# A recurrence block on one core: other durations in the books of the planner that orders its instructions

## The chip, the core and the metric

The kernel runs on one core of one Trainium2 chip, as one program with one launch. The metric is the device time of the execution in microseconds (us); the time before is the median of three runs. A profile is one further execution, taken by the hardware profiler.

## What is computed

The reference takes x of shape 8 x 1024 x 128 and applies two layers, each as `x = x + layernorm(layer(layernorm(x)))`. The first is a gated recurrence with 16 heads, keys of 64 and values of 128:

```
q, k, v = silu(causal_conv4(x @ W.T))          # per head; q, k then divided by their length
alpha   = exp(-exp(A_log) * softplus(x @ Wa.T + dt_bias));  beta = 2 * sigmoid(x @ Wb.T)
each token:  S = alpha * (S - beta * k (k S)) + k v ;  o = q S
result  = rms_norm(o) @ Wo.T
```

The second is a small feed-forward: two mixes of the token with the one before it, `sigmoid(mix_r @ W_r.T) * (square(relu(mix_k @ W_k.T)) @ W_v.T)`. All of it is in float32.

## The kernel before

**Tiling.** A unit is one batch entry (8), one half of its 1024 tokens (2) and one group of four heads (4): 64 units. A unit has four chunks of 128 tokens. Within a chunk the recurrence is written as matrix products: products of k with k and with q, weighted with decays (`products`, line 876); the inverse of a 128 x 128 triangular matrix for each head and chunk, 16 in a unit, made in blocks of 16 on GpSimd (`blocks`, line 957) and then from 16 to 32, 64 and 128 on TensorE, VectorE and ScalarE (`levels`, line 1002); and, chunk after chunk, the update of the state S (`prepares`, line 1119, and `steps`, line 1157). Ahead of this stand the normalisation of x and the gates (`begins`, 603), the projections with their convolutions (`conv`, 700, used by `keys`, 732, and `values`, 797) and the lengths of q and k (`lengths`, 740). Behind it stand the norm of the output with squares that accumulate (`norms`, 1233), the output projection (`projects`, 1263) and the second layer (`ending`, 1299).

**What sets the order.** All of these are generators, called streams, 17 in all. A stream runs to its next `yield part(...)`, which names the engine of the part that follows, the tiles that it reads, and the buffers and PSUM banks that it takes. `Flow.run` (line 177) holds the next part of each stream. For each it works out from its own books the time at which the part could start: the later of its engine's clock, of its operands' times plus SLACK (0.65) and of the time at which the buffers are free. Of those that could start within NEAR (0.35) of the earliest it takes the one of the lowest step number, and its instructions are issued. So the planner runs while the program is built, and what it leaves is a fixed order of instructions on each engine. On the chip each engine takes its instructions in that order, and waits where an operand isn't there.

The books are `Engine.cost` (line 245), which gives a duration for each instruction, and `Flow.note` (line 125), which moves the engine's clock on by it and marks when tiles were written and read. For TensorE the cost also has two shares of use, from which `Flow.clock` (line 106) works out windows in which TensorE's clock is halved; in such a window `run` puts parts with a low share off (YIELD). A DMA is booked with 3.0 us and half a microsecond of its queue (ISSUE). No number of the books reaches the program except through the order.

**PSUM.** Two tiles of two banks (pair) and four of one bank (bank) serve all products. A group of products writes one of them; the next group mostly writes another.

**The chain of the inverse.** `gathers` (line 936) writes the diagonal blocks of 16 of mt to DRAM in eight DMAs (md), and reads them back with the factors (cb, nb). `blocks` first multiplies nb with cb and then runs 28 small operations with tmp and nb on GpSimd. `scatters` (line 982) sends the result through DRAM (td) into tq, from which `levels` starts. In `levels` the tile x64 (x in the profile) is made on VectorE and tt on ScalarE. GpSimd also fills the first three columns of pb for the convolutions, whose taps follow on VectorE as acc.

Every instruction that the planner issues is recorded at line 234, the one call in `emit`, so the profile's groups are told apart by the names of their tiles. A float32 matmul leaves two records and a transposition one, so four products show as x8.

Of the kernel before, what the change touches and what calls it, by code (L numbers as in the profile page):

```python
# [22 lines left out]
NB = CU * G  # L23
# [11 lines left out]
class Flow:  # L35
# [11 lines left out]
    NEAR = 0.35  # L47
    SLACK = 0.65
    ISSUE = 0.5
    WINDOW, SLEEPS, WAKES = 3.4133, 0.475, 0.75  # L50

    def __init__(self, nc):
        self.now = dict(PE=0.0, DVE=0.0, ACT=0.0, POOL=0.0, SP=0.0)
        self.free, self.wrote, self.read = {}, {}, {}
        self.kinds, self.work = {}, [0.0, 0.0]
        self.of = {}
        self.speed, self.window, self.used = 1.0, self.WINDOW, [0.0, 0.0]
        self.pe, self.ve = Engine(self, "PE", nc.tensor), Engine(self, "DVE", nc.vector)
        self.ac, self.po = Engine(self, "ACT", nc.scalar), Engine(self, "POOL", nc.gpsimd)
        self.sp = Engine(self, "SP", nc.sync)  # L60
# [45 lines left out]
    def clock(self, t, cost, use):  # L106

        left = cost
        while True:
            while self.window <= t:  # L110
                if self.speed == 1.0:
                    if self.used[0] < self.SLEEPS * self.WINDOW:
                        self.speed = 0.5
                elif self.used[1] >= self.WAKES * self.WINDOW:
                    self.speed = 1.0
                self.used = [0.0, 0.0]
                self.window += self.WINDOW
            if left < 1e-6:
                return t
            d = min(left / self.speed, self.window - t)  # L120
            left -= d * self.speed
            self.used = [u + d * k for u, k in zip(self.used, use)]
            t += d

    def note(self, eng, op, outs, ins, cost):
        t = self.now[eng]
        for ap in ins:
            t = max(t, self.last(self.wrote, ap, eng))
        for ap in outs:
            if ap.space != DRAM:  # L130
                t = max(t, self.ends(ap, eng))
        if eng == "PE":
            self.now[eng] = self.clock(t, *cost)
            self.work = [self.work[0] + cost[0], self.work[1] + cost[0] * cost[1][1]]
            end = self.now[eng] + 0.1 + 0.1 / self.speed
        elif eng == "SP":
            self.now[eng] = t + self.ISSUE
            end = t + cost
        else:
            self.now[eng] = end = t + cost  # L140
        for ap in ins:
            self.mark(self.read, ap, end, eng)
        for ap in outs:
            self.mark(self.wrote, ap, end, eng)
# [79 lines left out]
class Engine:  # L224
# [20 lines left out]
    def cost(self, op, outs, ins, args, kw):  # L245
        def size(ap):
            n = 1
            for k in list(ap.shape)[1:]:
                n *= k
            return n  # L250

        n = size(outs[0])
        if self.name == "PE":

            if op == "transpose":
                return 0.109, (0.88, 0.88)
            k, m = ins[0].shape[0], size(ins[0])
            if n <= 4:
                return (0.08 if n == KW - 1 else 0.223), (0.0, 0.0)
            if k <= 32 and m <= 32:  # L260
                return 0.011 + 0.0005 * n, (0.0, 0.0)
            if k <= 64 and m <= 64:
                return 0.105, (0.64, 0.04)
            if m <= 32:
                return 0.25, (0.5, 0.2)
            t = max(0.223, n * 0.00168)
            return (t, (1.0, 1.0)) if k > 64 and m > 64 else (0.58 * t, (1.0, 0.58))
        if self.name == "DVE":
            if op == "tensor_tensor_scan":
                return 0.23 + 0.00204 * n  # L270
            if op == "bn_stats":
                return 0.28
            if op == "bn_aggr":
                return 0.18
            if op == "tensor_scalar" and n == P:
                return 0.38
            if op == "scalar_tensor_tensor":
                return 0.23 + (0.00117 if all(ap.space != PSUM for ap in ins) else 0.00104) * n
            return 0.155 + 0.00104 * n
        if self.name == "ACT":  # L280
            if "accum_out" in kw:
                return 0.174 + 0.0008 * n + 0.23
            if n == TU and op == "activation":
                return 0.69 if kw.get("scale") is not None else 0.63
            return 0.175 + 0.0008 * n
        if self.name == "POOL":
            if ALU.pow in args:
                return 0.41 + 0.166 * n
            if op == "memset":
                return 0.12  # L290
            if op == "tensor_scalar":
                return 0.25 + 0.0009 * n
            return 0.33 + 0.0018 * n
        return 3.0
# [1131 lines left out]
```

## Time and profile before

| | |
|---|---|
| median of 3 runs | 3776.48 us (3766.68 to 3783.44) |
| the profiled execution's own time | 3780.87 us |
| its span, first to last instruction | 3779.1 us |
| mean granted TensorE clock | 0.949 of full speed |
| HBM read and written | 138.18 MB and 23.07 MB, 43 GB/s over the span |
| DMA, mean of its largest queue | 22.9% of 16 engines' span |

The busy time of an engine is the time in which at least one of its instructions was executing, and its share is of the span. The chain of waits starts at the last instruction and goes back, at each step, to what released it; its shares add up to the span. An entry such as "DVE acc" stands for VectorE (DVE) writing the tile acc; ACT is ScalarE, POOL is GpSimd, SP is SyncE, which issues the DMAs, and PE is TensorE. A timeline's row gives the start and the length in us, the engine, the operation, the tile written and those read, the count of records, and in brackets the idle time of the engine before it with what ended it.

### The profile page before, as it was taken

To read this page: it belongs to the slowest core of one execution; us is meant where nothing else is said; L and a number is where in the kernel's file an instruction comes from. 1 tells how busy PE (TensorE), PEld (TensorE's weight loads), DVE (VectorE), ACT (ScalarE), POOL (GpSimd) and SP (SyncE) were. 2 spreads that over 40 slices of the span, in tenths; PEclk is the share of its full clock that TensorE was granted. 3 is DMA by queue.
4 is the path that set the end of the run, shared out by engine and by line. 5 is a ranking of instruction groups with operands and counts; after the bars stand their busy time and mean duration, and the time that the engine had idled before them with its cause. 6 is when DMAs were issued, how large, how long until landed. Compare 5 with 4: busy or idle time off the path is not lost.

```text
span 3779.1 us, 126912 instructions
## 1 busy us (share of the span) xinstructions
PE 3435.4 (91%) x52848; PEld 2646.7 (70%) x52848; DVE 2688.5 (71%) x5021; ACT 2311.7 (61%) x5779; POOL 2404.3 (64%) x4369
## 2 busy tenths in 40 slices
PE   6899998999999999998998989999998989989996
PEld 3677776777777776776766767767776767667775
DVE  5776767677777777866777677777767777777752
ACT  4566656666657666666656656566565666566652
POOL 4666667567666666666566566666666656576662
PEclk8899999999999999999999999999999989999997
DMA  3221222222222222221222222222222222222210
GB/s 80 56 53 39 54 45 49 54 45 55 49 55 46 57 50 43 56 53 40 54 44 53 52 42 53 47 54 51 51 45 55 49 41 60 44 48 53 49 39 11
DMA packets 713151, 186.28 MB, mean 49 GB/s; under 512 B 573152, under 2 KB 679040, under 8 KB 712576
## 3 DMA queue, kind: packets, MB, share of 16 engines
q1 hardware_dynamic: 712576, 178.17, 22.9%
q8 instruction: 415, 6.80, 0.8%
q14 instruction: 160, 1.31, 0.1%
HBM read 138.18 MB, written 23.07 MB: 43 GB/s over the span
## 4 chain that ended last, share of the span: by engine, by line
PE 63%; DVE 10%; POOL 7%; ACT 7%; SPq 6%; issue 5%; DMA 3%; POOLq 0%; DVEq 0%; ACTq 0%
PE bank L234 38%; PE pair L234 25%; SPq L234 6%; DVE acc L234 5%; POOL nb L234 3%; POOL tmp L234 2%; DMA nb<-md 2%; ACT acc L234 1%; DVE x L234 1%; ACT tt L234 1%; DVE at L234 1%; ACT L234 1%; ACT pb L234 1%; POOL vr L234 1%; ACT junk L234 1%
## 5 line engine op out<-in xcount | busy, mean ns | idle before, releaser
L234 DVE SCALAR_TENSOR_TENSOR acc<-pb,taps,acc 128x512 f32<-128x512 f32 x1344 | 1076.1, 806 | 158.2 <-POOL pb L234 64.9
L234 POOL TENSOR_TENSOR vr<-vr,r 128x128 f32<-128x128 f32 (+1 forms) x448 | 353.9, 791 | 252.5 <-ACT vr L234 247.0
L234 PE MATMUL bank<-xnT,wT 128*128 128x512 f32 x892 | 492.4, 641 | 14.8 <-ACT tt L234 8.7
L234 POOL TENSOR_TENSOR nb<-nb,tmp 128x14 f32<-128x14 f32 (+6 forms) x896 | 337.8, 377 | 70.2
L234 ACT COPY pb<-bank 128x512 f32<-128x512 f32 x446 | 259.6, 582 | 161.0 <-PE bank L234 122.1
L234 POOL TENSOR_TENSOR qk<-qk,egb 128x256 f32<-128x256 f32 x256 | 228.4, 892 | 202.5 <-PE pair L234 201.4
L234 ACT COPY o<-pair 128x512 f32<-128x512 f32 x256 | 150.4, 588 | 328.3 <-PE pair L234 286.2
L234 POOL TENSOR_TENSOR tmp<-nb 128x14 f32<-128x14 f32 (+6 forms) x896 | 319.4, 356 | 48.4
L234 DVE TENSOR_TENSOR_SCAN at<-at,ident 128x512 f32<-128x512 f32 x256 | 336.5, 1314 | 12.0 <-DMA at<-rowd 11.7
L234 PEld LDWEIGHTS bank<-tn,mt 32*32 32x32 f32 (+1 forms) x14240 | 276.4, 110 | 97.1 <-issue 22.3
L234 ACT ACTIVATE junk<-o 128x128 f32<-128x128 f32 x1024 | 317.5, 310 | 26.4
L234 PE MATMUL bank<-tn,mt 32*32 32x16 f32 (+1 forms) x14240 | 310.0, 190 | 17.8 <-DVE tn L234 7.6
L234 PE MATMUL pair<-vr,tt 128*128 128x128 f32 x2048 | 292.9, 289 | 26.7 <-ACT tt L234 19.5
L234 ACT ACTIVATE acc<-bank,taps 128x512 f32<-128x512 f32 x446 | 309.7, 694 | 0.3
L234 POOL TENSOR_TENSOR so<-so,es 128x4 f32<-128x4 f32 x256 | 64.2, 251 | 377.7 <-ACT junk L234 377.4
L234 PE MATMUL bank<-woT,oT 128*128 128x128 f32 x2048 | 290.1, 285 | 10.5 <-ACT oT L234 7.2
L234 PEld LDWEIGHTS bank<-wv,xnT 128*128 128x128 f32 x2016 | 257.9, 197 | 57.8 <-issue 36.1
L234 POOL TENSOR_TENSOR o<-o,so 128x512 f32<-128x512 f32 x256 | 284.8, 1112 | 18.0
L234 PEld LDWEIGHTS pair<-vr,tt 128*128 128x128 f32 x2048 | 265.9, 203 | 42.6 <-ACT tt L234 22.1
L234 PE MATMUL pair<-w,at 128*128 128x128 f32 x2048 | 291.8, 287 | 0.2 <-issue 0.2
L234 PE MATMUL bank<-wv,xnT 128*128 128x128 f32 x2016 | 284.7, 286 | 7.4 <-issue 3.5
L234 PEld LDWEIGHTS bank<-woT,oT 128*128 128x128 f32 x2048 | 255.2, 194 | 46.0 <-issue 15.9
(202 smaller groups left out, 7739.1 us busy)
## 6 DMA issues: line engine op xcount, KB each, us to landing
at<-rowd SPq DMA_DIRECT2D x256, 256.0 KB, 3.3
egb<-rowd SPq DMA_DIRECT2D x512, 64.0 KB, 3.2
tq<-td SPq DMA_DIRECT2D x256, 64.0 KB, 2.2
tt<-tq SPq DMA_DIRECT2D x256, 64.0 KB, 2.6
md<-mt SPq DMA_DIRECT2D x512, 16.0 KB, 1.8
nb<-md SPq DMA_DIRECT2D x64, 128.0 KB, 2.8
td<-nb SPq DMA_DIRECT2D x128, 64.0 KB, 3.1
xs<-in_L_attn_x_dram SPq DMA_DIRECT2D x16, 256.0 KB, 3.4
```

Source lines behind the costliest of these rows:

```text
L234: res = call(*args, **kw)
```

## The change

Other numbers are put into `Engine.cost`, and `Flow.note` adds a time whenever a TensorE instruction writes another tile than the one before it. The streams, their step numbers and offsets, HOP, SLACK, NEAR, YIELD, the shares of use and the entries of the other operations stay. Here n is the number of columns written and NB is 16.

```diff
@@ class Flow
+    TURN = 0.07
...
+        self.into = None
@@ note
         if eng == "PE":
+            if outs[0].tensor.name != self.into:
+                self.into, t = outs[0].tensor.name, t + self.TURN
             self.now[eng] = self.clock(t, *cost)
@@ cost, TensorE
             if op == "transpose":
-                return 0.109, (0.88, 0.88)
+                return 0.115, (0.88, 0.88)
...
-            t = max(0.223, n * 0.00168)
-            return (t, (1.0, 1.0)) if k > 64 and m > 64 else (0.58 * t, (1.0, 0.58))
+            t = max(0.235, n * 0.00172)
+            return (t, (1.0, 1.0)) if k > 64 and m > 64 else (0.61 * t, (1.0, 0.58))
@@ cost, VectorE, operations without an entry of their own
-            return 0.155 + 0.00104 * n
+            return (0.23 if n <= 2 * NB else 0.155) + 0.00104 * n
@@ cost, ScalarE
             if "accum_out" in kw:
-                return 0.174 + 0.0008 * n + 0.23
+                return 0.174 + 0.0008 * n + 0.33
```

## The prediction

> **What bounds the kernel.** I read the page's spans first, then its slices, its chain of waits, and then the timeline around single idle times of TensorE.
>
> ```profile
> span 3779.1 us, 126912 instructions
> PE 3435.4 (91%) x52848; PEld 2646.7 (70%) x52848; DVE 2688.5 (71%) x5021; ACT 2311.7 (61%) x5779; POOL 2404.3 (64%) x4369
> ...
> PE 63%; DVE 10%; POOL 7%; ACT 7%; SPq 6%; issue 5%; DMA 3%; POOLq 0%; DVEq 0%; ACTq 0%
> ```
>
> The reader is to see that TensorE is the bound but not all of it: it is idle for 3779.1 - 3435.4 = 344 us, and 37% of the chain runs through the other engines and the queues. The mean granted clock, 0.949, hides a third part: the trace's clock is either whole or half, so the half clock held for about 2 x 0.051 x 3779 = 386 us, in 62 stretches, and cost at most 193 us.
>
> TensorE's own work at full clock I add up from paces read as start to next start in the timeline: 4,224 products of 128x128 at 0.223 us, 464 of 128x512 at 0.86, 3,584 with one side 64 at 0.134, 1,024 of 64x256 at 0.258, 2,831 transpositions at 0.109, 13,312 of 32x32 (8,192 at 0.0186, 5,120 at 0.035), 2,048 of 64x64 at 0.10, 256 against the 32-column pair at 0.25 and some 20 us of small ones: 3,014 us. The order has 3,983 changes of the tile written, and four products take 0.893 us without one and 0.987 with: 0.094 each, 374 us. Together 3,388 us. So about 372 us between TensorE's groups are stalls and half clock, and 19 us are start and end. A schedule can win or lose only in the 372 and in the number of changes.
>
> How a stall is made is seen in the timeline of TensorE, VectorE, ScalarE and GpSimd around 1840 us (start, length, then the group; in brackets the idle time before it):
>
> ```profile
> 1839.07 1.02 PE L234 MATMUL bank<-xnT,wT 128*128 128x512 f32 x2
> 1842.50 0.44 PE L234 MATMUL bank<-ident,qk 128*128 128x128 f32 x2 [2.41 <-ACT tt L234]
> ...
> 1846.78 1.92 PE L234 MATMUL pair<-vr,tt 128*128 128x128 f32 x8
> ...
> 1857.12 1.06 PE L234 MATMUL pair<-vr,tt 128*128 128x128 f32 x8
> ```
> ```profile
> 1838.70 2.41 DVE L234 SCALAR_TENSOR_TENSOR acc<-pb,taps,acc 128x512 f32<-128x512 f32 x3 [1.65 <-POOL pb L234]
> 1841.14 0.69 DVE L234 TENSOR_TENSOR x<-bank,cn 64x512 f32<-64x512 f32 x1
> ```
> ```profile
> 1837.32 0.73 POOL L234 TENSOR_TENSOR nb<-nb,cb 128x256 f32<-128x256 f32 x1 [2.04 <-DMA nb<-md]
> ```
>
> Read it from below: GpSimd waits 2.04 us for a DMA; behind it in its queue stands the filling of pb; VectorE's taps wait for pb, and x of the levels stands behind the taps; ScalarE's tt waits for x; TensorE waits 2.41 us. Then the clock is halved: the same eight records take 1.92 us instead of 1.06. An in-order queue that waits for something later than the planner thought is the mechanism, and the DMA's duration in the books (3.0) isn't edited.
>
> **The change, part by part.** No instruction of work is added or removed: both built programs hold the same products, operations, DMAs and table loads; bare waits rise by 24 in all (TensorE -27, VectorE +32, ScalarE +11, SyncE +15, GpSimd -7), at most some 2 us at the 0.07 us that GpSimd's timeline shows between two instructions, and beside other work. I take 0 for them. What moves is the order, everywhere: from the 17th run of TensorE's order on the two differ, and of 7,066 runs 2,702 still follow each other alike. At large nothing moves: TensorE's groups of the recurrence stand on average 2 to 3 us of TensorE work earlier (spread 3), the convolutions 0.3 later; only the gates' products of begins stand 58 us later, which still has begins done ahead of need.
>
> TensorE's entries. Four products: books 0.892 before, 0.94 + 0.07 = 1.01 after, trace 0.987. One of 128x512: 0.860, 0.951, trace 0.97 with the change of tile. Four of one side 64: 0.517, 0.643, trace 0.55 to 0.65. Four transpositions: 0.436, 0.53, trace 0.44 to 0.53. Summed over all instructions the books held 2,962 us for TensorE and hold 3,110 + 3,948 x 0.07 = 3,386 now, against my 3,388. So TensorE's books were 13% short and now are right. The other two entries are less so: a square with accumulator is booked at 0.606 instead of 0.506, while two in a row start 0.43 to 0.44 us apart (1,024 of them, 102 us too much on ScalarE); small VectorE operations of 16 columns go from 0.172 to 0.247, while their rows show 0.163 to 0.253 (384 of them, 29 us). These cost no time themselves; they act through the order alone.
>
> The order. The changes of tile fall from 3,983 to 3,948: 35 x 0.094 = 3.3 us gained. For the stalls I counted, in both orders, how much TensorE work (at the paces above) stands between a group and the last earlier TensorE group on which its operands or its free bank depend, through other engines and everything ahead in their queues. Call it the cover. Set beside the trace of before, the excess time ahead of groups (idle and half clock together) falls with it: 186 groups had under 1 us and lost 129 us, 0.69 each; 431 had 1 to 1.75 us and lost 117 us, 0.27 each; 832 had 1.75 to 2.5 and lost 88, 0.106 each; 2,534 had more and lost 39, 0.015 each. In the new order these counts are 145, 552, 817 and 2,434. So -41 x 0.69 = -28.3, +121 x 0.27 = +32.9, -15 x 0.106 = -1.6, -100 x 0.015 = -1.5: +1.5 us. The worst places get fewer, the middling ones more, as a planner should do that no longer counts TensorE work short: it fits a wait more closely, with less left over.
>
> The DMA chain isn't in that count, since what waits is GpSimd. The cover between the products that feed md and GpSimd's first operation on nb falls from 14.9 to 14.4 us on average over the 64 units. Bounds: nothing, or 0.53 x 64 = 34 us of GpSimd's waiting. I take nothing: in the trace of before the wait on nb doesn't get longer with less cover (correlation +0.2, the wrong sign), since the DMAs stand in SyncE's queue behind others.
>
> At the half clock a rule can be weighed. The trace has 62 half-clock stretches, and ahead of 60 of them TensorE was idle for over 30% of 3.4 us, though only 22 idle times are over 3 us; at 1842.50 one of 2.41 us was enough. My prices per group hold the half clock already, from the rows. The Trainium skill (TensorE: Matmul & The Clock Gate, HAM oscillation) gives as its rule that TensorE should have no idle gaps over some 3.4 us, so that shorter ones would cost only themselves. By it the prices would be those of the groups at full clock, 0.42, 0.185, 0.047 and nothing, and the orders would differ by -17.2 + 22.4 - 0.7 = +4.5 us instead of +1.5; the rows of this trace go against the rule, and the sum goes by the rows.
>
> Sum: -3.3 + 1.5 = -1.8 us on the profiled execution's 3780.9 (span 3779.1 and 1.8 around it): 3779. That execution lies 4.4 us over the median of 3776.5, so I forecast 3775.
>
> **The rivals.** Faster: the groups with 1 to 1.75 us lost 0.27 each because the old books misjudged them; where the new books put 121 more, the work does fit, and they cost nothing. For it: TensorE's sum is now right to 0.1%. Against: the example's stall began at a DMA, not at a wrong product. Then -28.3 - 1.6 - 1.5 - 3.3 = -35: 3742. It is over 0.5% (19 us, about what a measurement here can tell from no change) if such a place costs under 0.13.
>
> Slower: thinner cover over the DMA chain decides. Place: GpSimd's first operation of blocks, behind nb.
>
> ```profile
> POOL nb L234 <- DMA nb<-md: 87.3, 49, 5.5
> ```
>
> It waits in 49 of 64 units already (total, times, longest). DMA nb<-md holds 2% of the chain, 76 us, so 0.87 of that waiting is felt at the end. If the lost cover becomes waiting one for one, 34 x 0.87 = 30 us; and each idle us has drawn 193 / 344 = 0.56 us of half clock: 46 us. With -1.8 that is 3821. It decides for slower by 0.5% as soon as 40% of the 34 us is felt. The correlation speaks against it, the example's timeline for it.
>
> That the change does nothing, because the planner would pick the same, is excluded by the orders.
>
> **How the numbers follow.** Within 0.5%, which is the forecast's own range of 3758 to 3795: 0.36, the likeliest, at 3775, where the places priced by before balance. Slower: 0.34, at 3821 and between, since a tighter order has less in hand for any operation that comes late. Faster: 0.30, at 3742. The price per place is a mean over few: ten more or fewer deep stalls of 1 to 3 us with their half clock are 15 to 45 us, either way. The range takes in both rivals and that spread beyond them by about 15 to 27 us: 3715 to 3835.
>
> **What would show it.** TensorE's busy time less its half clock falls by 3 us and no more. Idle times of TensorE over 1 us, 103 now: about as many if I am right, under 90 in the faster case. The wait of GpSimd on DMA nb<-md, 87.3 us: over 110 in the slower case. The clock stays at 0.945 to 0.953; 0.96 says faster, 0.94 slower. I am wrong if the page shows another engine's share of the chain grow by over 3% of the span, since then a queue that I did not count decides.

## The result, and the profile after

The changed kernel takes **3814.07 us** (median of 4 runs, 3812.62 to 3826.56) beside 3771.87 for the kernel before on the same chip (four runs there, the three of the table and one more): 1.0104 times as long, 95% interval 1.0081 to 1.0128. I had forecast 3775 and no change. The time lies inside the range, 3715 to 3835, but the likeliest case was wrong. The profiled execution took 3812.86 us.

From the page after, the span, the engines and the chain of waits:

```profile
span 3811.1 us, 126936 instructions
PE 3444.4 (90%) x52848; PEld 2644.8 (69%) x52848; DVE 2701.8 (71%) x5021; ACT 2308.7 (61%) x5779; POOL 2421.4 (64%) x4369
...
PE 51%; POOL 13%; DVE 10%; SPq 7%; ACT 6%; issue 5%; DMA 5%; POOLq 0%; DVEq 0%; ACTq 0%
```

The counts of instructions of work are those of before. The span is 32 us longer: TensorE is idle for 23 us more (3811.1 - 3444.4 = 366.7, before 343.7) and busy for 9 more. The half clock isn't the reason: it held for 364 us in 54 stretches (before 388 in 62), and the mean granted clock rose from 0.949 to 0.953.

**Where the time went.** I put both traces on one scale, TensorE's own work done at the full-clock paces of the prediction, and took the difference of the times at which the same amount of work was done. Over the first 2,510 us of work the difference wanders between -15 and +18 us; from 2,420 on it stays between 0 and 10. Over the next 40 us of work, from 2,788 us of time in the kernel after, it jumps by 30; close to the end it stands at +37.8, and the spans differ by 32.0. So the loss that is left at the end has one place. Fifty microseconds around it, in the windows of before and after (length, then busy us of PE, PEld, DVE, ACT, POOL, then granted clock, DMA share and GB/s):

```profile
2755.00:2805.00 50.00, 47.68 (x791) 37.22 (x788) 34.93 (x62) 30.75 (x82) 35.33 (x63) 0.97 0.26 49
```
```profile
2800.00:2850.00 50.00, 35.46 (x563) 23.20 (x559) 39.29 (x55) 24.45 (x50) 33.66 (x71) 0.81 0.28 51
```

TensorE is busy for 35 us there instead of 48, and part of that at half clock. What it lacks is seen from SyncE's queue: the blocks of the inverse of one unit, number 47 of 0 to 63, the last unit of the sixth of eight batch entries. First before, then after:

```profile
2624.26 0.55 SPq L234 DMA_DIRECT2D rowd<-rows  x1
...
2747.03 3.77 SPq L234 DMA_DIRECT2D md<-mt  x8
...
2752.18 0.40 SPq L234 DMA_DIRECT2D nb<-md  x1
...
2773.81 1.33 SPq L234 DMA_DIRECT2D td<-nb  x2
```
```profile
2769.66 0.38 SPq L238 DMA_DIRECT2D rowd<-rows  x1
2771.53 0.33 SPq L238 DMA_DIRECT2D at<-rowd  x1
...
2776.64 3.93 SPq L238 DMA_DIRECT2D md<-mt  x8
...
2783.84 0.52 SPq L238 DMA_DIRECT2D nb<-md  x1
...
2811.70 1.32 SPq L238 DMA_DIRECT2D td<-nb  x2
```

The eight DMAs that carry the unit's blocks start 30 us later than before, though the two traces were at most some 9 us apart in the 75 us of work ahead of that, the result goes out 38 us later, and `levels` starts at 2,821 instead of 2,786. The lines just ahead of the DMAs say why: rowd<-rows writes the decays of the *next* batch entry to DRAM, at<-rowd reads them back, and only then do the products of unit 47's last chunk go. Before, the same write stood 123 us ahead of the unit's DMAs. The longest wait of SyncE's queue in this stretch, 2,690 to 2,830 us (total, times, longest):

```profile
SPq L238 <- DVE rows L238: 24.3, 1, 24.3
```

A long wait there is no sign by itself, since before the queue waited 19.2 us for another tile (cr) in the same stretch; what counts is what stood behind it. TensorE's rows from the gates of the next entry to the starved stretch:

```profile
2718.32 1.87 PE L238 MATMUL bank<-wabT,xnT 128*128 128x32 f32 x16
...
2768.78 0.27 PE L238 MATMUL bank<-ident,al 128*128 128x128 f32 x1
...
2820.92 1.75 PE L238 MATMUL bank<-tn,mt 32*32 32x16 f32 x128 [2.84 <-DVE tn L238]
...
2842.46 1.12 PE L238 MATMUL bank<-ident,vT 128*128 128x128 f32 x4 [5.23 <-ACT vT L238]
```

The last rows of the next entry's gates pass TensorE at 2768.78; a microsecond later the DMA to rowd goes. They stood 4.0 us of TensorE work ahead of the last chunk of unit 47; in the order before it was 123.

**The mechanism, from the code.** In `products` a chunk fetches the decays of the *next* chunk (`fetch`, after the scan) before it issues its own products on TensorE. At the last chunk of an entry's last unit the next chunk belongs to the next entry, so `fetch` waits on `when=lambda: b in gs`, that is until `begins` has finished that entry. `begins` counts its step number so that the last parts of an entry's gates stand some 7 steps above the last chunk that waits for them: other parts that could start go first. With TensorE booked longer the planner sees less idle time on it, so `begins` is picked late; that reason is argued from the code, but the orders bear it out. On average over the seven changes of entry the gates stand 83 to 115 us of TensorE work ahead of the chunk in the six orders of the experiments below that keep the old entries of TensorE, to the last digit or so, and leave `begins` alone (the kernel before, squares alone, small operations alone, three null edits), and 29 to 66 in the five with the new entries (the kernel after, TensorE's entries alone, three null edits). I call what follows a late chunk: the products of the 7th entry's gates start at 2,533 us before and at 2,718 after. The last chunk then starts 35.9 us after the one before it, where 4 to 11 are usual. Its gathers, GpSimd's blocks and `levels` follow; the other streams run out of work for TensorE meanwhile, and the unit's first update of the state comes 95 us after that of the unit before it (before 53).

### The profile page after: what moved, and what is told of

The parts are those of the page before. It is cut to its first block, busy times and chain, and to the rows that moved or that the text cites. A ratio compares the mean times of both kernels' runs of the same rounds, so it can differ in the third digit from the quotient of the medians.

```text
span 3811.1 us, 126936 instructions
## 1 busy us (share of the span) xinstructions
PE 3444.4 (90%) x52848; PEld 2644.8 (69%) x52848; DVE 2701.8 (71%) x5021; ACT 2308.7 (61%) x5779; POOL 2421.4 (64%) x4369
## 4 chain that ended last, share of the span: by engine, by line
PE 51%; POOL 13%; DVE 10%; SPq 7%; ACT 6%; issue 5%; DMA 5%; POOLq 0%; DVEq 0%; ACTq 0%
PE bank L238 29%; PE pair L238 22%; SPq L238 7%; DVE acc L238 5%; POOL nb L238 4%; POOL tmp L238 3%; DMA nb<-md 2%; POOL vr L238 2%; DVE at L238 1%; ACT acc L238 1%; DVE x L238 1%; ACT tt L238 1%; ACT junk L238 1%; POOL o L238 1%; DVE mt L238 1%
## 5 line engine op out<-in xcount | busy, mean ns | idle before, releaser
L238 DVE SCALAR_TENSOR_TENSOR acc<-pb,taps,acc 128x512 f32<-128x512 f32 x1344 | 1091.8, 819 | 219.6 <-POOL pb L238 117.8
L238 POOL TENSOR_TENSOR qk<-qk,egb 128x256 f32<-128x256 f32 x256 | 237.3, 927 | 254.2 <-PE pair L238 253.5
L238 PEld LDWEIGHTS bank<-tn,mt 32*32 32x32 f32 x14304 | 285.5, 112 | 111.4 <-issue 34.8
L238 POOL TENSOR_TENSOR tmp<-nb 128x14 f32<-128x14 f32 (+6 forms) x896 | 329.5, 368 | 48.0
L238 PE MATMUL bank<-tn,mt 32*32 32x16 f32 x14304 | 320.3, 191 | 27.1 <-DVE tn L238 11.8
L238 DVE TENSOR_TENSOR mt<-pair,at 128x512 f32<-128x512 f32 x256 | 175.7, 686 | 225.3 <-PE pair L238 160.7
L238 PE MATMUL bank<-wv,xnT 128*128 128x128 f32 x2024 | 286.6, 286 | 25.9 <-ACT tt L238 15.7
L238 POOL TENSOR_TENSOR o<-o,so 128x512 f32<-128x512 f32 x256 | 294.3, 1150 | 18.0
L238 PE MATMUL pair<-qk 64*128 64x256 f32 x2048 | 280.7, 393 | 8.0 <-ACT o L238 4.9
```

The costliest lines, as they stand in the source:

```text
L238: res = call(*args, **kw)
```

## The experiments

Each ratio is to the kernel before, run beside it on the same chip, with its 95% interval. The kernel before took 3772 to 3789 us on these chips, so the ratios compare better than the times. Two accounts run through the expectations: the "jam", in which a late chunk holds up what follows, and "thin cover", in which the many middling places of the prediction's count cost the time. "Late" is the time from the start of the second last chunk's products to that of the last. A "jump" is the rise of the difference to the kernel before within 45 us of TensorE work at that place, of the profiled executions. Taken as the largest rise over any 45 us of work near the place, the jumps of the table below come out up to 4 us larger; with no time at all counted for a change of tile, the one of the kernel after is still 31.

**Take the coupling away.** The last chunk of an entry no longer fetches across entries.

```diff
-                if k < len(units) * CU:
+                if k < len(units) * CU and units[k // CU][0] in gs:
```

> The changed kernel, but products no longer fetches the decays of the next batch entry before it has issued its own last chunk, as long as that entry's gates aren't planned. Up to the seventh entry the order is the same as the changed kernel's. The place where the changed kernel lost some 28 us in one unit was TensorE's products of the last chunk of unit 47 standing 35.7 us of TensorE work behind those of the chunk before, where 5 to 10 are usual; here they stand 6.0 behind. Theory of the jam: 3814 less 25 to 31, so 3783 to 3789, and the unit that took 45 us longer is gone. Rival, cover spread thin over the whole run: the counts of cover are as good as those of the changed kernel (150, 535, 852, 2409), so 3810 to 3818.

Measured: 3815.45, 1.0105 (1.0074 to 1.0135); its profiled execution took longer than its timed ones, 3836. A miss in the time. Unit 47's last chunk is no longer late (5.9 us), and the jump there is gone. But with that wait gone nothing makes the planner pick `begins` either: the gates of the 7th entry now come 17 us and those of the 8th 53 us *after* the last chunk that used to wait for them, the first update of unit 56 comes 103 us after that of unit 55 (57 before), and there is a jump of 15.6 there (24 as the largest rise near the place). The wait went to the next entry's own first chunk. So the fetch is only where the lateness is felt; the late `begins` is its source.

**Put the late gates into the kernel before.** `begins` of the 7th entry may start three units of `keys` later; all up to there stays.

```diff
-    when=lambda: prog["keys"] >= (b - 1) * NH * NG + 3 or b == 0)
+    when=lambda: prog["keys"] >= (b - 1) * NH * NG + (6 if b == 6 else 3) or b == 0)
```

> The kernel before with its old books, but the gates of the seventh batch entry may begin only three units of keys later. The order is the same as before up to that entry; then the products of the last chunk of unit 47 stand 38.2 us of TensorE work behind the chunk before (8.2 in the kernel before). Theory of the jam: 25 to 35 us slower than before, 3797 to 3807, all of it lost in units 47 and 48. Rival, thin cover: the counts are those of before within a few (188, 460, 840, 2487), +8 us by their prices: 3776 to 3784.

Measured: 3816.10, 1.0097 (1.0073 to 1.0121), more than expected. The gates stand 4.1 us ahead, the last chunk is 40.5 late, and the jump at the same place is 32.4; at every 300 us of work up to 2,120 the two traces are within 4 us of each other. SyncE's queue and the window show the picture of after, with the old books:

```profile
2773.99 0.38 SPq L234 DMA_DIRECT2D rowd<-rows  x1
...
2780.53 3.76 SPq L234 DMA_DIRECT2D md<-mt  x8
...
2816.76 1.32 SPq L234 DMA_DIRECT2D td<-nb  x2
```
```profile
2805.00:2855.00 50.00, 33.56 (x537) 22.16 (x537) 32.21 (x49) 23.11 (x49) 34.53 (x75) 0.79 0.25 44
```

One late chunk is enough for the whole loss, without any of the change.

**Take the late gates out of the kernel after**, in that entry alone: in `run`, `begins` counts as eight steps earlier while b is 6.

```diff
-   could.append((at, steps[s][0], k))
+   could.append((at, steps[s][0] - (self.early if s.__name__ == "begins" else 0.0), k))
...
+   flow.early = 8.0 if b == 6 else 0.0
```

> The changed kernel, with one thing moved: the step number of begins counts 8 lower for the seventh batch entry alone. The order is that of the changed kernel up to there; then the gates stand 96 us of TensorE work ahead of the last chunk of unit 47 instead of 4, and that chunk 5.0 behind the one before instead of 35.7. Theory of the jam (late gates): the 25 to 30 us of the one place go, 3780 to 3790. If what cost the time is spread over the run, or if the jam only moves on as in the run without the fetch across entries: 3805 to 3820.

Measured: 3777.03 beside 3782.57, 0.9991 (0.9973 to 1.0009), 3 us under the jam's forecast. The last chunk is 4.9 us late with the gates 100 us ahead, and the jump is gone. From its timeline of SyncE's queue, its windows and its chain:

```profile
2745.37 4.78 SPq L239 DMA_DIRECT2D md<-mt  x8
...
2773.16 1.73 SPq L239 DMA_DIRECT2D td<-nb  x2
```
```profile
2765.00:2815.00 50.00, 48.77 (x795) 37.75 (x791) 35.87 (x60) 32.95 (x84) 27.53 (x50) 0.97 0.27 53
```
```profile
PE 53%; POOL 12%; DVE 10%; ACT 8%; SPq 6%; issue 5%; DMA 4%; POOLq 0%; DVEq 0%; ACTq 0%
```

The starved window is full again, while GpSimd still holds 12% of the chain, as after, at the time of before. So the chain's shares moved with the order and don't price the loss. Two edits in opposite directions, each leaving the order up to the place alone, agree: **the pair's loss is this late chunk.**

**All gates earlier** in the kernel after, by the offset of `begins`, 1.60 to -0.40:

```diff
-   (weights(), 1000, 0.0), (begins(), 4.75, 1.60), ...
+   (weights(), 1000, 0.0), (begins(), 4.75, -0.40), ...
```

> The changed kernel with begins planned two units earlier (offset -0.40 instead of 1.60), which moves the whole order. Late last chunks: none over 17.5 us of TensorE work (16.6 and 17.5, otherwise 4 to 8), so about 20 us of jam in place of 28. Cover: 124, 486, 876 and 2,466 places, at the prices that the changed kernel paid 376 us instead of 408. Theory of the jam alone: 3800 to 3810. Both theories together: 3765 to 3785. Thin cover alone: 3775 to 3790. Neither: 3814.

Measured: 3759.94, 0.9947 (0.9928 to 0.9967), faster than both kernels and than every forecast named. No jump over 13 anywhere; the latest chunks are 16.6 and 15.7. The page:

```profile
span 3754.4 us, 126917 instructions
PE 3414.2 (91%) x52848; PEld 2624.9 (70%) x52848; DVE 2702.9 (72%) x5021; ACT 2315.5 (62%) x5779; POOL 2426.5 (65%) x4369
```

TensorE's busy time is 30 us shorter than after, at a clock of 0.959. With the small operations of VectorE alone (0.9949, below) it is the fastest of these orders, but what follows says how little the last half per cent means.

**Each part of the change alone.** The entries of TensorE with the time for a change of tile:

> The new TensorE entries alone; squares and small VectorE operations as before. Its order has four late last chunks instead of one: 39.5, 29.7, 30.6 and 18.9 us of TensorE work behind the chunk before, in the first, fourth, sixth and seventh change of batch entry. Theory of the jam: (39.5 + 29.7 + 30.6 + 18.9) less 4 x 7 usual = 91 us, at about one us lost for each as in the changed kernel: 3850 to 3870, so slower than the changed kernel though its TensorE entries are the same. Rival, thin cover: 123, 577, 827 and 2,412 places at the prices that the changed kernel paid (0.66, 0.33, 0.106, 0.018) make 402 us instead of 408: 3800 to 3812.

Measured: 3873.99, 1.0246 (1.0223 to 1.0268), a little over the jam's forecast and far over that of thin cover. Four of the seven changes of entry have late chunks, by 42.2, 29.2, 31.5 and 18.9, and there the jumps are 33.6, 29.2, 25.7 and 12.5 (together 101; the profiled executions differ by 93). The squares with accumulators alone (`+ 0.23` to `+ 0.33`):

> The kernel before with the new entry for squares alone. No last chunk stands late (13.2 us of TensorE work at most, gates 64 to 158 ahead), counts of cover 161, 449, 850, 2,490, at before's prices 11 us fewer than before and 3 us of tile changes fewer. Theory of the jam and counts: 3758 to 3772. Rival, the overpriced square is what misleads the planner: over 3795.

Measured: 3825.33, 1.0119 (1.0071 to 1.0167). A miss, in the range of the rival: no late chunk over 16.5, and yet a loss, 48.7 us by 1,520 us of work, 21.8 of it at one place (245), and 37 at the end. The small operations of VectorE alone:

> The kernel before with the new entry for small VectorE operations alone. No last chunk late (10.6 at most, gates 60 to 101 ahead); counts 157, 476, 865, 2,478, at before's prices 5 us fewer. Theory of the jam and counts: 3765 to 3780, the same as before. Rival, this entry brings the loss: over 3795.

Measured: 3767.36, 0.9949 (0.9927 to 0.9970). The parts don't add up (2.46 + 1.19 - 0.51 = 3.1%, the whole 1.04%): each makes a new order, none carries a price of its own.

**More slack.** SLACK 0.75 instead of 0.65 in the kernel after, so that the counts of thin cover fall; it also ends the late chunk.

> The changed kernel with SLACK at 0.75 instead of 0.65, so that the planner leaves 0.1 us more between an operand's time and its use. The whole order moves. No last chunk late (8.2 at most, gates 41 to 86 ahead); counts of cover 116, 445, 860, 2,548: fewer of the tightest than in any of these, and at before's prices 41 us fewer than before. Theory of the jam and counts together: 3730 to 3750, faster than both kernels. The jam alone, without a part for thin cover: 3770 to 3790. Rival, right TensorE entries are bad for this planner whatever else: over 3800.

Measured: 3789.93, 1.0016 (0.9998 to 1.0034). The jam's forecast held to the edge; the cover's missed by 40 us. The thin places did get fewer, but the excess ahead of TensorE's groups fell only to 387.5 us, where prices times counts say about 331: a place that is left costs more.

**Gates early, by another rule.** `begins` counts as eight steps earlier in all entries (`- (8.0 if s.__name__ == "begins" else 0.0)`), with TensorE's entries alone and with the whole change:

> The new TensorE entries alone, as in the run that took 3874, with begins counted 8 steps lower for every batch entry. No last chunk late any more: 7.8 us of TensorE work at most behind the chunk before, gates 94 to 153 ahead. Theory of the jam: the 90 to 100 us go, 3765 to 3785. Rival, right TensorE entries thin the cover and cost time whatever begins does: 3820 or more.

> The changed kernel with begins counted 8 steps lower for every batch entry. No last chunk late (12.1 at most, gates 95 to 143 ahead); counts of cover 116, 471, 861, 2,495, the fewest tight places of all orders with SLACK as it is. Theory of the jam, and counts at before's prices (35 us fewer than before): 3735 to 3760, faster than both kernels. The jam alone: 3765 to 3785. Rival, the new books cost time of themselves: over 3800.

Measured: 3832.88, 1.0117 (1.0094 to 1.0141), and 3810.22, 1.0058 (1.0041 to 1.0076). The jam's forecast missed both, and both times lie in the range of its rival, that the new entries cost time whatever `begins` does. No late chunk is over 11.2 and no jump at a change of entry over 15, and the first is 1.3% faster than TensorE's entries without the early gates; but a drift of 51 and 40 us by 1,520 us of work stays. That doesn't show the rival's reason, since edits that correct nothing cost as much:

**Edits that correct nothing.** Of the kernel before, VectorE's scan at 0.231 for 0.230, a transposition at 0.1095 for 0.109, NEAR at 0.36 for 0.35:

> The kernel before, its scan booked at 0.231 + 0.00204 n instead of 0.230: a thousandth of a microsecond, which corrects nothing but makes the planner break ties otherwise. One last chunk stands late by this (23.3 us of TensorE work behind the chunk before, at the fifth change of entry, gates 3.0 ahead); counts of cover 182, 469, 794, 2,500, at before's prices 3 us more. Theory of the jam: 10 to 20 us slower than before, lost there, 3785 to 3800. If right or wrong durations were what decides: 3770 to 3785, as before.

> The kernel before, its transposition booked at 0.1095 instead of 0.109. No last chunk late (8.2 at most, gates 60 to 150 ahead); counts 168, 457, 838, 2,510, at before's prices 6 us fewer. Theory of the jam: as before, 3765 to 3785. If any new order scatters by 1% (as the run with the squares alone may say), it can lie anywhere from 3740 to 3820.

> The kernel before with NEAR at 0.36 instead of 0.35, which corrects nothing and makes a new order throughout. No last chunk of a batch entry stands more than 8.2 us of TensorE work behind the one before it. If late chunks were the whole of what separates orders: 3765 to 3785, as before. If orders scatter for other reasons too, as the two earlier edits without a real change did (3835 with a late chunk, 3821 without): anywhere in 3760 to 3835, and a time over 3790 speaks for a kernel before that is a lucky draw among its like.

Measured: 3835.32, **1.0129** (1.0110 to 1.0148); 3820.95, **1.0094** (1.0073 to 1.0115); 3794.51, **1.0038** (1.0021 to 1.0056). The jam's forecast missed the first by 35 us, with a jump of only 16.2 at its late chunk, and the second, which has no late chunk, by 36. And of the kernel after the scan at 0.231, a transposition at 0.1155, NEAR at 0.36:

> The kernel after with VectorE's scan booked at 0.231 instead of 0.230. Three last chunks of batch entries are late in its order, by 16.6, 25.7 and 14.7 us of TensorE work (5 to 10 is usual), with the next entry's gates 5 us ahead of each. By the jam: 20 us or so at the 25.7 and less at the other two, 3800 to 3830. If a late chunk cost nothing beyond its own pair of kernels: the scatter alone, 3760 to 3800.

> The kernel after with a transposition booked at 0.1155 instead of 0.115. Two last chunks are late, by 33.0 and 29.1 us. By the jam: a jump of 25 to 35 us in the time against the kernel before at each of these two places, and 3810 to 3850. If a late chunk cost nothing: 3760 to 3800, with no jump there.

> The kernel after with NEAR at 0.36 instead of 0.35. No last chunk is late (at most 5.9 us). By the jam as what sets the new books' loss: 3760 to 3790, no more than the kernel before, and without a jump over 12 us at a change of entry. If the new books' orders are worse for another reason: 3800 to 3830, as in the kernel after with all gates 8 steps early (3810).

Measured: 3795.34, **1.0029** (1.0007 to 1.0052); 3865.22, **1.0221** (1.0206 to 1.0237); 3854.33, **1.0191** (1.0168 to 1.0215). These three carry the change as well; to the kernel after, at 1.0104, they stand at about -0.7%, +1.2% and +0.9%. The first is 5 us under the jam's forecast, the second 15 over its own. The second has its two late chunks and its jumps there; SyncE's queue at the first of them, at 850 to 960 us:

```profile
SPq L238 <- DVE rows L238: 26.9, 1, 26.9
```

The third missed all that was named: no late chunk, and the third largest loss of all.

**What a late chunk costs.** Every chunk over 18 us late, in six orders; the jump is 0.64 to 1.0 of the lateness, 0.80 on average:

| order | entry change | late, us | jump, us |
|---|---|---|---|
| TensorE's entries alone | 1st | 42.2 | 33.6 |
| before, gates late | 6th | 40.5 | 32.4 |
| after | 6th | 35.9 | 30.3 |
| after, transposition 0.1155 | 2nd | 33.4 | 30.4 |
| TensorE's entries alone | 6th | 31.5 | 25.7 |
| after, transposition 0.1155 | 5th | 30.8 | 23.0 |
| TensorE's entries alone | 4th | 29.2 | 29.2 |
| before, scan 0.231 | 5th | 25.4 | 16.2 |
| after, scan 0.231 | 5th | 25.0 | 20.0 |
| TensorE's entries alone | 7th | 18.9 | 12.5 |

Those of 14.8 to 16.6 show no jump over 13. So the price holds in orders that it wasn't derived from. It isn't the whole time of an order: other jumps over 12 us (up to 26) stand away from any change of entry, so the smallest of the table could be scatter, and some of what is lost comes back later. Without the jumps of this table the profiled executions of the three null edits of before lie +45, +51 and +1 us from it, the kernel after +2, and its null edits -5, +38 and +77.

The new entries do bring late chunks more often: in the 35 changes of entry of the five orders with TensorE's new entries that were named above there are eight over 18 us, in the 42 of the six with the old ones there is one.

## Why the prediction was wrong, point by point

- **The step that failed**: "only the gates' products of begins stand 58 us later, which still has begins done ahead of need". 58 us is a mean over the entries. The distance between the gates and the last chunk that needs them is, at the seven changes of entry, 52, 23, 80, 49, 70, **4** and 42 us of TensorE work after (127, 142, 145, 61, 121, 123 and 84 before). A mean lead of 46 says "ahead of need"; the smallest says "no". The planner itself waited there, so it could have been read from the order before any run: the last chunk of the sixth entry stands 35.7 us of TensorE work behind the one before it, those of the others 4 to 12.
- **TensorE's work**: changes of tile -3.3 us. The 0.094 us was read at the wrong event. In the trace of before, at full clock:

```profile
559.43 1.06 PE L234 MATMUL pair<-w,at 128*128 128x128 f32 x8
560.32 1.06 PE L234 MATMUL pair<-vr,tt 128*128 128x128 f32 x8
561.22 1.06 PE L234 MATMUL bank<-woT,oT 128*128 128x128 f32 x8
562.20 0.72 PE L234 MATMUL pair<-S,pT 64*128 64x128 f32 x8
```

  Each group writes another tile than the one before it, but only where the next has blocks of another shape (64x128 for 128x128) is the start 0.98 us later, otherwise 0.89 or 0.90. Over the whole trace four products of 128x128 take a median of 0.893 us with a change of tile on both sides and the same shape (295 groups), and 0.987 before another shape in the *same* tile (84 groups). So the price belongs to the change of shape. The order has 2,523 of these before and 2,536 after, so this term was some 1 to 3 us of loss (13 at 0.094, and up to 0.1 more for the first product behind the change, 0.325 instead of 0.223) instead of 3.3 of gain; and TURN is booked at 1,644 changes of tile before, 1,641 after, that cost nothing, and not at 185 and 230 changes of shape within a tile. That the new books came to 3,386 against 3,388 was luck of the sum; group by group they are not right. The sign that I had named, busy time, can't show a term of this size (3444.4 beside 3435.4), since it holds the half clock and the waits inside a group.
- **The cover, +1.5 us**. The counts were right, since they are counts of the order. The prices after: 0.66 us for a place under 1 us (0.69 taken), 0.33 for 1 to 1.75 (0.27), 0.106 for 1.75 to 2.5 (0.106), 0.018 for more (0.015). With these the groups' excess, on the prediction's scale of work, is 408 us instead of 372, 35 more: the middling places cost 552 x 0.06 = 33 more than priced. But that is not a cause beside the late chunk: 28 of the 35 arise within the one place. And the counts don't carry over to other orders, as the kernel with more slack showed. They describe an order; they don't forecast one.
- **The DMA chain taken as nothing.** GpSimd's wait for nb rose by 19.4 us, from 87.3, under the 110 named for the slower case; VectorE's wait for pb rose as well, from 64.9. The page's waits after (total, times, longest):

```profile
POOL nb L238 <- DMA nb<-md: 106.7, 45, 5.1
...
DVE acc L238 <- POOL pb L238: 117.8, 84, 4.2
```

  Neither decides. In the kernel after with one gate early they are 107.1 and 111.8, at the time of before. So the slower rival's 3821 came close to 3814 by luck, by another mechanism than its own: the chain md, nb, td was late because its first link was issued late, not because of little cover behind it.
- **The faster rival** (places of 1 to 1.75 us free) fell: they cost 0.33 each.
- **The signs.** Idle times of TensorE over 1 us: 103, as forecast; the clock 0.953, within the forecast. Both agreed with no change while the time rose, so neither could see one place of 30 us. Nor did each idle microsecond draw 0.56 us of half clock, as the slower rival had it: TensorE's idle time rose by 23 us and the half clock fell by 24. GpSimd's share of the chain did grow by over 3%, from 7 to 13%, the sign that I had named for being wrong; but it stayed at 12% when the loss was taken away.
- **The clock rule** of the Trainium skill (TensorE: Matmul & The Clock Gate, HAM oscillation) would have made the sum 3 us larger; the loss was elsewhere, and no run here tells those 3 us. The rows after go against it as those before did: 54 half-clock stretches beside 18 idle times over 3 us.
- **What the forecast of no change left out** is the scatter. I gave 15 to 45 us for deep stalls either way, and centred it on the time before. The runs put the kernel before at the good end of it: the six null edits, which nothing was aimed at, were all slower than it, by 0.3 to 2.2%, the change included in three of them. The four orders with the old books (before and three null edits) lie on average 0.65% above the kernel before, with a spread of 0.57%, the four with the new ones 1.36%, with 0.87%. With four each that tells no difference, 0.71 with an uncertainty of 0.52. Whether better books make better orders stays open, the more as the entry for a change of tile wasn't better; that these didn't make the next order better is shown.

**Still open**: what the drift of orders without a late chunk consists of. It is seen in squares alone, in the transposition at 0.1095, in both kernels with gates eight steps early (40 to 51 us by 1,520 us of work in these four, 17 to 45 by 2,000) and in NEAR at 0.36 after (46 by 1,520, 77 at the end). It shows as idle time of TensorE, which over the 18 profiles rises from 331 to 400 us along with the time (correlation 0.95), and as half clock (311 to 463 us); what releases TensorE there isn't one thing. Neither the counts of cover nor the waits for nb and pb order the runs by time: the waits for nb are 100.7 us in the fastest order, 101.2 in one of the slowest (NEAR 0.36 in the kernel after) and 102.6 in the slowest.

## What to carry to other kernels

When a planner's books change, look in the new order for the one operand that arrives later than its use, by the *smallest* lead at each hand-over between outer iterations and not by the mean: a prefetch across the boundary makes the last piece of work of the old iteration wait for the first of the new. Then price the place by its lateness, of which about 0.8 was felt here.

Before a price is put into the books, find the event that it belongs to: hold the supposed cause and change the rest. Groups that change the tile and keep the shape would have shown that 0.094 us belongs to the shape.

Before a gain or loss of 1% is put down to better or worse numbers, run the same kernel with a number changed in its last digit. Here that alone moved the time by +0.4 to +1.3% from the kernel before and by -0.7 to +1.2% from the kernel after; a change of books in a greedy planner is judged over several such draws, not by one.

## What the runs showed of the hardware that I had not expected

The mean granted clock and the time need not move together: the kernel after runs at 0.953 and the one before at 0.949, yet it takes 1% longer. A change of the tile written costs no time here (0.893 us for four products of 128x128), and a change of the block's shape costs 0.094 us in the last product ahead of it, in the same tile too (0.987), and some 0.1 in the first behind it (0.325 for 0.223). And gates that pass TensorE 4 us ahead of a chunk instead of 123, seen as a wait of 24.3 us on SyncE's queue, starve TensorE some 20 to 75 us later, on the far side of two round trips of DMA and GpSimd's blocks; where TensorE's own idle times stand (2,790 to 2,845), nothing names its cause.
